# A conditional residual adapter on one core: b2 redistributed, and ScalarE's and VectorE's orders edited

## The chip, the cores and the metric

The kernel runs on one core of one Trainium2 chip. A core has several engines that work side by side, each with its own instruction queue that runs in order: TensorE (PE, matrix products and transposes, with PEld its weight loads), VectorE (DVE), ScalarE (ACT), GpSimd (POOL), and SyncE (SP), which here issues most DMA transfers. They wait for each other by semaphores. Data lies in SBUF; TensorE writes to PSUM, which has eight banks. The metric is the device time of one execution in microseconds (us).

## The reference

For each of 128 batches, x[b] is a matrix of 128 positions by 512 features. A language id picks one of ten adapters:

```
v = itok[b]
h = relu(x[b] @ W1[v] + b1[v])            # 128 x 128
y = x[b] + (h @ W2[v] + b2[v])            # 128 x 512
n = (y - mean(y)) / sqrt(var(y) + 1e-5)   # over the 512 features
out[b] = x[b] + n * gamma[v] + beta[v]
```

All inputs and the output are float32. The tables b2, gamma and beta hold values of their own, so none of these additions may be left out.

## The kernel before

**Set-up.** All tables are brought to SBUF once. W2 lies there for all languages. W1 lies there twice: w1e (lines 159 to 161, two loads) is used for the batches below 24, w1 for the rest (four loads, issued in iterations 12 to 18). The first eight batches have their W1 loaded directly (load_first). The rows of beta, gamma and b2 are spread over 128 partitions by small bf16 matmuls (spread), giving beta_b, gamma_b and b2_b.

**Main loop.** It starts on line 518. Iteration i works on several batches at once, since the steps of a batch are spread over iterations:

- TensorE: transpose_x(i) (four transposes, line 232), down(i-1) (four float32 matmuls, eight in the trace, line 255), up(i-2) (one float32 matmul, two in the trace, line 272). The product of down goes to the one bank of pool p_h, the transposes to the one of p_x, up to one of five banks of p_y, where ys[b] then stays to the end of its batch.
- ScalarE: copy_xT(i) (line 236), relu(i-1) (line 263), square(b) with b = i-3 (line 312; it also sums the squares), after each odd batch deviation (line 322: the root of the pair's variances), and last stage_w1(i+1) (line 223), which copies the W1 of a batch from w1e or w1 to a buffer of its own.
- GpSimd: add_b2 (line 242), r = x + b2, for most batches; add_beta (line 249), o = x + beta, for all.
- VectorE: residual(b) (line 289: y = up + r, with the row sum), and for batches done in pairs: negative_means (line 303), three Newton steps that turn the root into 1/standard deviation (lines 326, 328, 331), scale (line 355: (y - mean) * gamma) and finish (line 364: o = y * rstd + o). With p = g-1, the pair before the current one, the order is for an even batch: residual(b), Newton 1, scale(2p), Newton 2, finish(2p-1). For an odd batch: Newton 3, residual(b), scale(2p+1), negative_means(g), finish(2p).
- SP: loads of x, four batches at a time, and stores of two batches.

**Three ways for b2.** For most batches GpSimd adds b2 to x. For some, TensorE adds it by one more bf16 matmul into the same bank (b2_by_matmul, line 214; line 271 in the trace). For others VectorE adds it in place in a pass of its own (vector_b2, line 282), before residual. Before the change 94 batches go to GpSimd, 11 to TensorE and 23 to VectorE, these mostly four or eight batches apart.

**The order is written by hand.** The function keep (line 45) chains each instruction to the one before on the same engine, so that each engine's order is that of the Python program. Semaphore waits come from the tile framework: it makes an instruction wait for those that wrote what it reads, or that still use a buffer or bank that it takes over.

**Small results in PSUM.** One tile of 64 columns, small, holds a column pair of zeros (for negative_means) and all roots, in slots (smalls, line 295). The last four batches are done singly in tail (line 422), with deviation_of and rstd_of.

Of the kernel before, what the change touches and what calls it, by code (L numbers as in the profile page):

```python
# [8 lines left out]
FP = mybir.dt.float32  # L9
# [3 lines left out]
ALU = mybir.AluOpType  # L13
# [3 lines left out]
P = 128  # L17
G = 4
EPS = 1e-5
FIRST = 8  # L20
# [5 lines left out]
def cond_resid_kernel(ctx: ExitStack, tc: tile.TileContext, x, itok, W1, b1, W2, b2, gamma, beta, out):  # L26
# [8 lines left out]
    nc = tc.nc  # L35
    B, S, H = x.shape
# [8 lines left out]
    def keep(ins):  # L45

        engine = ins.ins.engine
        if engine in last:
            tc.add_manual_dep(ins.ins, last[engine], behind, reason="kept order")
        last[engine] = ins.ins.name  # L50
        return ins
# [7 lines left out]
    st = ctx.enter_context(tc.tile_pool(name="st", bufs=6))  # L59
    p_x = ctx.enter_context(tc.tile_pool(name="p_x", bufs=1, space=PSUM))  # L60
    p_h = ctx.enter_context(tc.tile_pool(name="p_h", bufs=1, space=PSUM))
    p_s = ctx.enter_context(tc.tile_pool(name="p_s", bufs=1, space=PSUM))
# [3 lines left out]
    E = B - 5  # L66
# [144 lines left out]
    xT, hT, rs, os, ys, ssqs, nmeans, rstds = {}, {}, {}, {}, {}, {}, {}, {}  # L211
    phs, pxs, sums = {}, {}, {}

    def b2_by_matmul(b):
        return b < 4 or (b % 4 == 1 and not b2_by_vector(b) and b < E)

    def b2_by_vector(b):
        return b % 4 == 1 and (b % 8 == 5 if b < 24 else b % 32 != 1) and 8 <= b < B - 8

    def stage_w1(b):  # L220
        w1s[b] = wp.tile([P, KC, A], FP, tag="w1s", name=f"w1s_{b}")
        src = (w1e if b < EARLY else w1).rearrange("p l k a -> p (l k a)")[:, bass.ds(lid(b, ET.Activation) * (KC * A), KC * A)]
        keep(nc.scalar.copy(w1s[b].rearrange("p k a -> p (k a)"), src))  # L223
# [10 lines left out]
    def copy_xT(b):  # L234
        xT[b] = tp.tile([P, KC, P], FP, tag="xT", name=f"xT_{b}")
        keep(nc.scalar.copy(xT[b], pxs.pop(b)))  # L236
# [42 lines left out]
    def vector_b2(b):  # L279
        if b2_by_vector(b):  # L280
            v = lid(b, ET.DVE)
            keep(nc.vector.tensor_tensor(ys[b], ys[b], b2_b[:, bass.ds(v * H, H)], ALU.add))  # L282

    def residual(b):
        r = rs.pop(b) if b in rs else xb(b)
        if b % 2 == 0:
            sums[b // 2] = st.tile([P, 2], FP, tag="sum", name=f"sum_{b // 2}")
        keep(
            nc.vector.scalar_tensor_tensor(ys[b], ys[b], 1.0, r, ALU.mult, ALU.add, accum_out=col(sums, b))  # L289
        )  # L290


    small = {}

    def smalls(lo, n):
        if not small:
            small["t"] = p_s.tile([P, 64], FP, tag="s", name="small")
            keep(nc.vector.memset(small["t"][:, 0:2], 0.0))
        return small["t"][:, lo : lo + n]

    def negative_means(g):
        nmeans[g] = st.tile([P, 2], FP, tag="nmean", name=f"nmean_{g}")
        keep(nc.vector.scalar_tensor_tensor(nmeans[g], sums[g], -1.0 / H, smalls(0, 2), ALU.mult, ALU.add))  # L303

    def square(b):

# [27 lines left out]

    def of_pair(g):
        if g not in parts_of:
            parts_of[g] = smalls(8 + 8 * (g % 2), 2), st.tile([P, 2], FP, tag="part", name=f"part_{g}")
        return parts_of[g]

    def deviation(g):  # L340
# [2 lines left out]
    def rstd(g, n):  # L343
        t, u = of_pair(g)
        if n < 3:
            newton(n, ssqs[g], t, u)
        else:
            rstds[g] = st.tile([P, 2], FP, tag="rstd", name=f"rstd_{g}")
            newton_3(rstds[g], t, u)
            del ssqs[g], parts_of[g]  # L350

    def scale(b):
        v = lid(b, ET.DVE)
        keep(
            nc.vector.scalar_tensor_tensor(  # L355
                ys[b], ys[b], col(nmeans, b), gamma_b[:, bass.ds(v * H, H)], ALU.add, ALU.mult
            )
        )
# [12 lines left out]
    def on(b):  # L371
        return 0 <= b < B
# [4 lines left out]

    def of_one(b):
        if -b not in parts_of:
            parts_of[-b] = smalls(32 + 8 * (b % 4), 1), st.tile([P, 1], FP, tag="part", name=f"part_of_{b}")  # L380
        return parts_of[-b]

    def rstd_of(b, n):

        t, u = of_one(b)
        if n < 3:
            newton(n, ssqs[b], t, u)
        else:
            rstds[b] = st.tile([P, 1], FP, tag="rstd", name=f"rstd_{b}")
            newton_3(rstds[b], t, u)  # L390

    def deviation_of(b):
        ssqs[b] = st.tile([P, 1], FP, tag="ssq", name=f"ssq_{b}")
        sq = tp.tile([P, H], FP, tag="sq", name=f"sq_{b}")
        keep(nc.scalar.activation(sq, ys[b], AF.Square, bias=col(sums, b), scale=-float(H), accum_out=ssqs[b]))
        root(ssqs[b], of_one(b)[0])
# [25 lines left out]
    def tail(b):  # L422
        p = E // 2
        residual(b)
        if b == E + 1:
            rstd(p, 1)
            scale(E - 1)
            rstd(p, 2)
            finish(E - 2)
            store(p - 1)  # L430
            rstd(p, 3)
            deviation_of(b)
            shift(E)
            by_pool(E, False)
        elif b == E + 2:
            rstd_of(b - 1, 1)
            negative_means(b // 2)
            rstd_of(b - 1, 2)
            finish_cols(E - 1)
            store_last(E - 1)  # L440
            rstd_of(b - 1, 3)
            store_last(E)
            deviation_of(b)
        elif b == E + 3:
            left, right = slice(0, H // 2), slice(H // 2, H)
            shift(b - 2)
            by_pool(b - 2, False)
            residual(b + 1)
            store_last(b - 2)
            rstd_of(b - 1, 1)  # L450
            scale(b - 1)
            rstd_of(b - 1, 2)
            negative_means(b // 2)
            deviation_of(b)
            scale(b)
            rstd_of(b - 1, 3)
            deviation_of(b + 1)
            by_pool(b - 1, True, left)
            rstd_of(b, 1)
            scale(b + 1)  # L460
            rstd_of(b, 2)
            finish_cols(b - 1, right)
            store_last(b - 1)
            rstd_of(b, 3)
            rstd_of(b + 1, 1)
            finish_cols(b)
            store_last(b)
            rstd_of(b + 1, 2)
            rstd_of(b + 1, 3)
            finish_cols(b + 1)  # L470
            store_last(b + 1)
# [46 lines left out]
    for i in range(3, B + U):  # L518
        b = i - U - 1
        if b > G and b % G == 2 and b // G + 3 < NG:  # L520
            load_x(b // G + 3)
        if i == 5:
            load_x(3)
        if i in (12, 14, 16, 18):
            load_w1((i - 12) // 2)
        if i == 4:
            up(2)
        if i == 5:
            up(3)
        if i > 3 and on(i):  # L530
            transpose_x(i)
        if b <= E:
            add_b2(b + 2)
            add_beta(b)
        if i > 4 and on(i - 1):
            down(i - 1)
        if i > 3 and on(i):
            copy_xT(i)
        if i > 4 and on(i - 1):
            relu(i - 1)  # L540
        if i > 5 and on(i - U):
            up(i - U)


        g, half = divmod(b, 2)
        p = g - 1
        mine, old = 0 <= p < B // 2, 0 <= p - 1 < B // 2
        if b == E:
            add_b2(b + 3)
            add_beta(b + 1)  # L550
            add_b2(b + 4)
            for n in range(b + 2, B):
                add_beta(n)
        if b > E:
            tail(b)
        elif half == 0:
            if on(b):
                residual(b)
            if mine:
                rstd(p, 1)  # L560
                scale(2 * p)
                rstd(p, 2)
            if old:
                finish(2 * p - 1)
                store(p - 1)
        else:
            if on(b):
                vector_b2(b)
            if mine:
                rstd(p, 3)  # L570
            if on(b):
                residual(b)
            if mine:
                scale(2 * p + 1)
            if on(b):
                negative_means(g)
            if mine:
                finish(2 * p)
        if 0 <= b <= E:
            square(b)  # L580
            if half == 1:
                deviation(g)
        if i + 1 >= FIRST and on(i + 1):
            stage_w1(i + 1)

        for n, engine in ((i + 3, ET.Activation), (i - U + 3, ET.PE), (b + 1, ET.DVE), (b + 5, ET.Pool)):
            if on(n):
                lid(n, engine)
# [37 lines left out]
```

## Time and profile before

| What | Value |
|---|---|
| Median of three runs | 311.27 us (310.89 to 311.38) |
| The profiled execution | 311.25 us |
| Its span in the trace | 309.4 us |
| PE busy | 298.0 us (96%) |
| DVE busy | 296.2 us (96%) |
| ACT busy | 280.1 us (91%) |
| POOL busy | 281.4 us (91%) |
| Matmuls of up, per matmul from the trace's group | 256, 598 ns |
| VectorE additions of b2 | 23, 692 ns each |
| Matmuls that add b2 | 11, 380 ns each |

The page gives each engine's busy time, a picture of the span in 40 slices where a digit is the busy share in tenths, the groups of instructions with their durations and idle time, and the waits. The durations of one instruction overlap those of the next, so steps are best read from start to start in the timeline: a matmul row's 275 or 598 ns is longer than the distance to the next matmul. A timeline row holds start, duration, engine, source line, operation, result and operands, and, in brackets, how long the engine was idle before it and which engine or transfer ended that. The granted TensorE clock was full in all stretches up to 300 us.

### The profile page before, as it was taken

The page shows a single profiled execution, that of the slowest core. Times are in us where ns is not written, and L with a number is a line of the kernel's source. Part 1 is how long each engine was busy: PE and PEld are TensorE (multiplying, and loading weights), DVE is VectorE, ACT ScalarE, POOL GpSimd, SP SyncE. Part 2 cuts the span into 40 slices and gives each one's busy share as a digit, 9 for nine tenths or more (in the row PEclk, how much of TensorE's full clock was granted, in tenths as well). Part 3 has the DMA queues.
Part 4 walks back from the last instruction along what each step waited for, and adds up shares of the span by engine and source line. Part 5 has one row for each costly group of instructions (what it writes and reads, how often), then busy time and mean ns, then how long its engine had stood idle before and what let it go on. Part 6 is the DMA issues. An engine that isn't in the chain of part 4 may idle for free. (4 is left out here: it accounts for less than half of the span.)

```text
span 309.4 us, 6966 instructions
## 1 busy us (share of the span) xinstructions
PE 298.0 (96%) x1845; PEld 222.1 (72%) x1845; DVE 296.2 (96%) x827; ACT 280.1 (91%) x716; POOL 281.4 (91%) x235
## 2 busy tenths in 40 slices
PE   8999999999999999999999999999999999999970
PEld 3758778787777777777777777777777777777740
DVE  6787999999999999999999999999999999999994
ACT  3857999999999999999999999999999999999991
POOL 1349999999999999999999999999999999999893
PEclk9999999999999999999999999999999999999995
DMA  7999979986677766666876766677765766882244
GB/s 232 390 387 387 374 225 370 375 278 232 230 271 267 243 210 225 222 233 239 271 249 219 246 202 246 228 250 271 249 225 203 244 237 222 263 271 106 111 159 170
DMA packets 43481, 77.58 MB, mean 251 GB/s; under 512 B 1930, under 2 KB 7061, under 8 KB 43443
## 3 DMA queue, kind: packets, MB, share of 16 engines
q1 hardware_dynamic: 43382, 77.10, 71.9%
q8 instruction: 15, 0.25, 0.3%
q14 instruction: 24, 0.19, 0.2%
q10 hardware_dynamic: 60, 0.05, 0.1%
HBM read 43.58 MB, written 33.55 MB: 249 GB/s over the span
## 5 line engine op out<-in xcount | busy, mean ns | idle before, releaser
L249 POOL TENSOR_TENSOR o<-x,beta_b 128x512 f32<-128x512 f32 x128 | 162.2, 1279 | 9.4 <-DVE beta_b L209 9.4
L255 PE MATMUL ph<-xT,w1s 128*128 128x128 f32 x1024 | 135.4, 275 | 0.0
L242 POOL TENSOR_TENSOR r<-x,b_b 128x512 f32<-128x512 f32 x94 | 120.2, 1279 | 13.1 <-DVE b_b L209 6.2
L272 PE MATMUL py<-w,hT 128*128 x256 | 132.0, 598 | 0.0
L255 PEld LDWEIGHTS ph<-xT,w1s 128*128 128x128 f32 x1024 | 124.9, 192 | 1.0 <-ACT hT L263 0.5
L232 PEld LDWEIGHTS pxT<-ident,x 128*128 128x128 f32 x512 | 66.6, 152 | 65.3 <-issue 35.4
L355 DVE SCALAR_TENSOR_TENSOR py<-py,nmean,gamma_b 128x512 f32<-128x512 f32 x126 | 95.0, 754 | 0.1
L364 DVE SCALAR_TENSOR_TENSOR o<-py,rstd,o 128x512 f32<-128x512 f32 x122 | 91.0, 746 | 0.0
L312 ACT ACTIVATE sq<-py,sum 128x512 f32<-128x512 f32 x124 | 85.2, 687 | 6.1 <-DVE py L289 6.1
L232 PE MATMUL pxT<-ident,x 128*128 128x128 f32 x512 | 78.0, 275 | 0.0
L236 ACT COPY xT<-pxT 128x512 f32<-128x512 f32 x128 | 75.1, 587 | 1.2 <-PE pxT L232 1.2
L289 DVE SCALAR_TENSOR_TENSOR py<-py,r 128x512 f32<-128x512 f32 x94 | 65.1, 693 | 1.4 <-PE py L272 0.7
L223 ACT COPY w1s<-w 128x512 f32 x104 | 63.6, 612 | 0.1
L263 ACT ACTIVATE hT<-ph,b1T 128x128 f32<-128x128 f32 x128 | 47.4, 370 | 6.4 <-PE ph L255 4.3
L272 PEld LDWEIGHTS py<-w,hT 128*128 128x128 f32 x256 | 39.6, 191 | 2.8 <-issue 0.9
L312 ACT ACTIVATION_READ_ACCUMULATOR sq<-py,sum 128x1 f32 x124 | 25.6, 206 | 0.0
L289 DVE SCALAR_TENSOR_TENSOR py<-py,x 128x512 f32<-128x512 f32 x34 | 23.8, 699 | 1.4 <-issue 0.8
L322 ACT ACTIVATE small<-ssq,eps 128x2 f32<-128x2 f32 (+1 forms) x66 | 17.5, 265 | 2.3 <-DVE nmean L303 0.2
L282 DVE TENSOR_TENSOR py<-py,b_b 128x512 f32<-128x512 f32 x23 | 15.9, 692 | 0.0
L289 DVE DVE_READ_ACCUMULATOR py<-py,r 128x1 f32 x94 | 13.3, 142 | 0.0
L326 DVE SCALAR_TENSOR_TENSOR part<-ssq,small 128x2 f32<-128x2 f32 x62 | 9.4, 152 | 1.8 <-ACT small L322 1.8
L223 ACT COPY w1s<-w1e 128x512 f32 x16 | 9.8, 613 | 1.2 <-DMA w1e<-in_L_cond_W_dram 1.1
(54 smaller groups left out, 97.4 us busy)
## 6 DMA issues: line engine op xcount, KB each, us to landing
out_dram<-o SPq DMA_DIRECT2D x61, 512.0 KB, 3.3
x<-in_x_dram SPq DMA_DIRECT2D x29, 1024.0 KB, 6.3
x<-in_x_dram SPq DMA_DIRECT2D x6, 512.0 KB, 8.9
w1e<-in_L_cond_W_dram SPq DMA_DIRECT2D x2, 1280.0 KB, 11.6
w<-in_L_cond_W_dram SPq DMA_DIRECT2D x4, 640.0 KB, 7.5
w1s<-in_L_cond_W_dram SPq DMA_DIRECT2D x8, 256.0 KB, 8.4
w<-in_L_cond_W_dram SPq DMA_DIRECT2D x1, 1792.0 KB, 10.1
out_dram<-o SPq DMA_DIRECT2D x6, 256.0 KB, 2.0
```

The costliest lines, as they stand in the source:

```text
L223: keep(nc.scalar.copy(w1s[b].rearrange("p k a -> p (k a)"), src))
L232: keep(nc.tensor.transpose(pxs[b][:, k, :], cols, ident))
L236: keep(nc.scalar.copy(xT[b], pxs.pop(b)))
L242: keep(nc.gpsimd.tensor_tensor(rs[b], xb(b), b2_b[:, bass.ds(v * H, H)], ALU.add))
L249: keep(nc.gpsimd.tensor_tensor(os[g][:, j, :], xb(b), beta_b[:, bass.ds(v * H, H)], ALU.add))
L255: nc.tensor.matmul(phs[b], lhsT=w1s[b][:, k, :], rhs=xT[b][:, k, :], start=(k == 0), stop=(k == KC - 1))
L263: keep(nc.scalar.activation(hT[b], phs.pop(b), AF.Relu, bias=b1T[:, bass.ds(lid(b, ET.Activation), 1)]))
L272: keep(nc.tensor.matmul(ys[b], lhsT=hT[b], rhs=w2[:, bass.ds(v * H, H)], start=not m, stop=True))
L289: nc.vector.scalar_tensor_tensor(ys[b], ys[b], 1.0, r, ALU.mult, ALU.add, accum_out=col(sums, b))
L312: nc.scalar.activation(sq, ys[b], AF.Square, bias=col(sums, b), scale=-float(H), accum_out=col(ssqs, b))
L355: nc.vector.scalar_tensor_tensor(ys[b], ys[b], col(nmeans, b), gamma_b[:, bass.ds(v * H, H)], ALU.add, ALU.mult)
L364: nc.vector.scalar_tensor_tensor(o, ys.pop(b), rstds[g][:, j : j + 1], o, ALU.mult, ALU.add)
```

## The change

Five edits are made together.

1. The batches are dealt out anew. From batch 24 on, of each sixteen batches three go to VectorE (those with remainder 1, 6 and 11) and one to TensorE (remainder 14). TensorE also gets batches 121 and 123. In all 93 batches go to GpSimd, 15 to TensorE and 20 to VectorE: 13, 21, 27, 33, 38, 43, 49, 54 and so on to 118. Six of the twenty are even batches, so vector_b2 is called for even batches, too, directly before residual.
2. ScalarE's order in an iteration becomes copy_xT(i), stage_w1(i+1), relu(i-1), square(b), deviation.
3. Each Newton step moves behind one more VectorE operation: Newton 1 behind scale(2p), Newton 2 behind finish(2p-1), Newton 3 behind residual of the odd batch.
4. The tile small and its memset are gone. negative_means takes the first two columns of ys[2g+1] as its second operand, with an operation that passes it by. Each root has a tile of its own in the one bank of p_s; those of batches 126 and 127 take the banks of p_h and p_x.
5. In the tail the first Newton step of batch 126 comes before the square of 127, and scale(127) moves behind Newton 3 of batch 126.

```diff
     def b2_by_matmul(b):
-        return b < 4 or (b % 4 == 1 and not b2_by_vector(b) and b < E)
+        return b in (0, 1, 2, 3, 5, E - 2, E) or (b % 8 == 1 if b < 24 else b % 16 == 14 and b < E)
 
     def b2_by_vector(b):
-        return b % 4 == 1 and (b % 8 == 5 if b < 24 else b % 32 != 1) and 8 <= b < B - 8
+        return 8 <= b < B - 8 and (b % 8 == 5 if b < 24 else b % 16 in (1, 6, 11))
...
-    small = {}
-
-    def smalls(lo, n):
-        if not small:
-            small["t"] = p_s.tile([P, 64], FP, tag="s", name="small")
-            keep(nc.vector.memset(small["t"][:, 0:2], 0.0))
-        return small["t"][:, lo : lo + n]
-
     def negative_means(g):
         nmeans[g] = st.tile([P, 2], FP, tag="nmean", name=f"nmean_{g}")
-        keep(nc.vector.scalar_tensor_tensor(nmeans[g], sums[g], -1.0 / H, smalls(0, 2), ALU.mult, ALU.add))
+        keep(
+            nc.vector.scalar_tensor_tensor(
+                nmeans[g], sums[g], -1.0 / H, ys[2 * g + 1][:, 0:2], ALU.mult, ALU.bypass
+            )
+        )
...
     def of_pair(g):
-            parts_of[g] = smalls(8 + 8 * (g % 2), 2), st.tile([P, 2], FP, tag="part", name=f"part_{g}")
+            parts_of[g] = p_s.tile([P, 2], FP, tag="s", name=f"root_{g}"), st.tile([P, 2], FP, tag="part", name=f"part_{g}")
...
     def of_one(b):
-            parts_of[-b] = smalls(32 + 8 * (b % 4), 1), st.tile([P, 1], FP, tag="part", name=f"part_of_{b}")
+            pool, tag = {E + 3: (p_h, "h"), E + 4: (p_x, "xT")}.get(b, (p_s, "s"))
+            parts_of[-b] = pool.tile([P, 1], FP, tag=tag, name=f"root_of_{b}"), st.tile([P, 1], FP, tag="part", name=f"part_of_{b}")
...
             rstd_of(b - 1, 3)
+            rstd_of(b, 1)
             deviation_of(b + 1)
             by_pool(b - 1, True, left)
-            rstd_of(b, 1)
-            scale(b + 1)
             rstd_of(b, 2)
             finish_cols(b - 1, right)
             store_last(b - 1)
             rstd_of(b, 3)
+            scale(b + 1)
...
         if i > 3 and on(i):
             copy_xT(i)
+        if i + 1 >= FIRST and on(i + 1):
+            stage_w1(i + 1)
         if i > 4 and on(i - 1):
             relu(i - 1)
...
             if on(b):
+                vector_b2(b)
                 residual(b)
             if mine:
+                scale(2 * p)
                 rstd(p, 1)
-                scale(2 * p)
-                rstd(p, 2)
             if old:
                 finish(2 * p - 1)
...
             if mine:
-                rstd(p, 3)
+                rstd(p, 2)
             if on(b):
                 residual(b)
             if mine:
+                rstd(p, 3)
                 scale(2 * p + 1)
...
-        if i + 1 >= FIRST and on(i + 1):
-            stage_w1(i + 1)
```

## The prediction

> **What bounds the kernel now.** I read the busy table first, then the slices, then the steps of TensorE (PE) in the timeline, then the waits. Busy shares do not decide: PE and VectorE (DVE) both stand at 96%, and for most of the span at nine tenths or more in every slice.
>
> ```profile
> PE   8999999999999999999999999999999999999970
> DVE  6787999999999999999999999999999999999994
> ```
>
> So I went to the starts of PE's own steps. Per batch it runs T (four transposes, L232), D (eight down matmuls, L255) and U (two up matmuls, L272).
>
> ```profile
> 100.72 1.02 PE L272 MATMUL py<-w,hT 128*128 x2
> ...
> 105.11 1.02 PE L272 MATMUL py<-w,hT 128*128 x2
> 105.97 0.60 PE L232 MATMUL pxT<-ident,x 128*128 128x128 f32 x4
> 106.40 1.06 PE L255 MATMUL ph<-xT,w1s 128*128 128x128 f32 x8
> 107.30 1.02 PE L272 MATMUL py<-w,hT 128*128 x2
> ```
>
> U to U is 6.58 us for three batches, 2.19 a batch: U to T 0.86, T to D 0.44, D to U 0.89 (rounded). From 37.0 to 130.5 us no step is longer than this, apart from T before batch 24 (0.47) and 0.22 for each matmul that adds b2 (91.74 to 91.96). PE is the limit there, and what delays it once there stays. After 130 us it stalls ten times, for instance here:
>
> ```profile
> 139.44 1.06 PE L255 MATMUL ph<-xT,w1s 128*128 128x128 f32 x8
> 140.41 1.12 PE L272 MATMUL py<-w,hT 128*128 x2
> 141.37 0.38 PE L232 MATMUL pxT<-ident,x 128*128 128x128 f32 x2
> ```
>
> D to U is 0.97 and U to T 0.96, so 0.17 is lost, 1.74 over all ten. DVE causes it: four batches take 8.94 (149.88 to 158.82) against PE's 8.76, until U must wait for a bank. Without the b2 addition (L282), which costs 0.67 more (155.41 to the residual at 156.14 is 0.73, where 0.06 stands otherwise), DVE needs 8.27 for four, 2.07 a batch. It falls behind by 0.67 at an addition and recovers 0.12 in each batch without.
>
> **Part 1: b2 dealt out.** Additions on DVE go from 23 to 20, matmuls that add b2 from 11 to 15, GpSimd additions from 94 to 93. DVE saves 3 x 0.67 = 2.0; six of the 20 now stand on even batches, where no Newton step fills the 0.06 between addition and residual, +0.4. These 1.6 are off the path unless DVE is the limit. PE gains 4 x 0.22 = **+0.88** (bounds 0, if all fell into waits, and 0.88; I take 0.88, since PE shows no wait there). With DVE at 16 x 2.07 + 3 x 0.67 + 0.06 = 35.2 per 16 batches and PE at 16 x 2.19 + 0.22 = 35.3, DVE no longer falls behind without end, and the old stalls go: **-1.74** (bounds -1.74 and 0). GpSimd keeps 28 additions per 16 batches, at 1.23 from start to start 34.5, and stays hidden behind PE's 35.3.
>
> **Part 2: the W1 copy ahead of ReLU.** The copy for batch 8 is the first from w1e, and it waits for that load.
>
> ```profile
> 28.22 0.58 ACT L236 COPY xT<-pxT 128x512 f32<-128x512 f32 x1
> 29.11 0.37 ACT L263 ACTIVATE hT<-ph,b1T 128x128 f32<-128x128 f32 x1 [0.31 <-PE ph L255]
> ...
> 31.26 0.62 ACT L223 COPY w1s<-w1e 128x512 f32 x1 [1.11 <-DMA w1e<-in_L_cond_W_dram]
> ```
>
> Today ReLU of batch 6 runs at 29.11, before the wait. Changed, the wait begins at 28.7 and stands in front of it, with square 4 and the next xT copy queued behind. The load was issued by SP at 17.6 and depends on nothing that moves. ReLU 6 starts at 31.26 + 0.52 = 31.78, ends at 32.15, and D of batch 7 may load weights 0.05 later, as it did at 25.69 after the ReLU ending at 25.64. A weight load that waits isn't overlapped: that D took 1.00 to the next U instead of 0.89.
>
> ```profile
> 25.69 1.16 PE L255 MATMUL ph<-xT,w1s 128*128 128x128 f32 x8
> 26.69 0.59 PE L272 MATMUL py<-w,hT 128*128 x1
> ```
>
> So D of batch 7 counts from 32.30, not 30.46: +1.84. The old kernel lost 0.35 right after (U at 31.35 takes 1.06, T at 32.41 0.58, T at 34.75 0.50), which goes. Net **+1.49**. Bounds: the page's median of 11.6 from issue to landing would put it at 29.6, which gives 0.2 - 0.35 = -0.15; a landing 0.1 later than today's gives 1.6. I take the wait's own row. In the steady loop the swap is neutral: the same instructions stand between a square and the next ReLU. SP's and GpSimd's queues keep their order, and every x load and store keeps its place.
>
> **Part 3: the mean reads the batch's own bank.** negative_means (L303) now names the first two columns of the odd batch's ys as an operand that it ignores. It takes 0.15 either way. But as built, the square of every odd batch waits for that mean, where it waited for the residual.
>
> ```profile
> 155.41 0.69 DVE L282 TENSOR_TENSOR py<-py,b_b 128x512 f32<-128x512 f32 x1
> ...
> 156.14 0.70 DVE L289 SCALAR_TENSOR_TENSOR py<-py,x 128x512 f32<-128x512 f32 x1
> ...
> 157.42 0.15 DVE L303 SCALAR_TENSOR_TENSOR nmean<-sum,small 128x2 f32<-128x2 f32 x1
> ```
>
> ```profile
> 156.93 0.69 ACT L312 ACTIVATE sq<-py,sum 128x512 f32<-128x512 f32 x1 [0.34 <-DVE py L289]
> ...
> 157.74 0.27 ACT L322 ACTIVATE small<-ssq,eps 128x2 f32<-128x2 f32 x1
> 157.94 0.60 ACT L223 COPY w1s<-w 128x512 f32 x1
> 158.45 0.57 ACT L236 COPY xT<-pxT 128x512 f32<-128x512 f32 x1
> 158.93 0.37 ACT L263 ACTIVATE hT<-ph,b1T 128x128 f32<-128x128 f32 x1
> ```
>
> Residual to square is 0.79 here. Changed it is 1.28 to the mean, 0.06 for the Newton step now in between, 0.15 for the mean and 0.04 of signal: 1.53. Behind the square on ACT come root, two copies and ReLU, and for that ReLU waits the D after next (one ph bank). Let U of the odd batch start at u. The residual starts at u + 1.13 if DVE is level (40.81 to 41.94), u + 1.86 with an addition ahead. Then square u + 3.39, ReLU 2.00 later at 5.39, weight load at 5.81, with 0.10 for the lost overlap D counts from 5.91. Unhindered it starts at 0.86 + 4.38 + 0.44 = 5.68: 0.23 lost. The old order gives 5.17, no loss. An even addition leaves the next odd batch 0.61 behind: 0.10 lost. Five batches of 0.12 and the stall bring DVE level before the next addition. Twelve odd ones from batch 24 on at 0.225, six even at 0.10, two earlier (slower T) at 0.135: 2.70 + 0.60 + 0.27 = **+3.57**. The old trace shows no such wait, so bounds: 0, if rows are 0.2 shorter than read, and 6.7, if each of the 31 other odd squares from batch 24 to 121 also costs a 0.10 overlap. The row of 0.10 itself is the nearest, so I keep 3.57.
>
> The Trainium skill, page "PSUM — Partial Sum Buffer", section on bank collisions, says that the compiler's scheduler adds a dependency between any two instructions of different engines on one bank, reads against reads included; that speaks against this edit. No row before shows two readers of one bank at once. Priced as a 0.15 instruction alone the edit is free and the sum is 311.85; with the rule's wait it is 315.4.
>
> **Part 4: Newton, root banks, tail.** The first Newton step moves behind scale. Its root, 0.74 later now, ends at residual + 2.6; the step stands at 2.06 + 0.61 + 0.66 = 3.3. No wait. A memset of 0.06 goes at 22.12, where DVE is ahead. A single root bank makes each root wait for the last Newton step of the pair before, which ends before the mean that its square awaits: nothing. In the tail the 0.45 wait at 302.71 (Newton of 126 behind the root of 127) ends, but finish of 125's right half then waits for ScalarE's left half, which by the same rows ends 0.1 earlier than today's 302.61 + 0.45; the work behind it fits as before: **-0.03**, bounds -0.6 (that wait not made) and +0.2.
>
> **Sum.** 311.25 (the profiled execution; span 309.4 and 1.85 around it; 0.02 under the median) + 0.88 - 1.74 + 1.49 + 3.57 - 0.03 = **315.4 us**, 1.3% slower.
>
> **Rivals.**
> A: odd squares don't reach PE. For it: 0.23 is small beside 5.7 of chain. Against: each link is a row. 311.25 + 0.88 - 1.74 + 1.49 - 0.03 = 311.85, at the upper edge of no change.
> B, the other side: DVE sets the pace (20.00 of 20.00 busy from 100 us on), PE's steps can shrink and absorb matmuls and waits. Then only DVE's 1.6 counts: 309.6. It decides if PE can run a batch under 2.19. Against it: 90 us without a shorter step.
> C: ACT becomes the limit, since its slack is small (two batches take it 4.19, 149.51 to 153.70, against PE's 4.38), and each odd square costs: 315.4 + 3.1 = 318.5.
>
> **Numbers.** Forecast 0.62, A 0.17, B 0.11, C 0.10. Its own range, with 0.1 either way at each of the 18 additions, is 313.6 to 317.2; to hold 8 in 10 it reaches over A: 310.9 to 317.4, which leaves out B and most of C. Under 0.2% (0.6 us) this kernel's measurement can't tell from no change: faster 0.12 (B and a little of A), same 0.12 (A), slower 0.76.
>
> **What would show it.** Right: w1s waits about 2.5 us on w1e, directly before a ReLU; waits "ACT sq <- DVE nmean" on odd batches; D with a first step 0.10 longer after odd additions; no D-to-U stretch of 0.97 after 130 us; 15 rows of L271's group. Wrong: T to T at 2.19 through odd additions (A), or under it (B). A landing of w1e near 29.6 would take 1.6 off.

## The result and the profile after

The changed kernel takes 314.99 us (median of four runs, 314.66 to 315.15) against 311.20 us for the kernel before on the same chip: a ratio of 1.0121, 95% interval 1.0104 to 1.0139. It is 1.2% slower. 315.4 was forecast. The profiled execution took 314.66 us, with a span of 312.9 us (309.4 before); lines after the edit are numbered one or a few apart from before (down is L256, up L273, square L309).

The slices of the busy table say no more than they did before: both engines are still at nine tenths nearly everywhere.

```profile
PE   7999899999999999999999999999999999999970
DVE  6877799999999999999999999999999999999995
```

The groups and the table of waits say more. Here a line of a group gives busy time and mean duration, then the idle time ahead of it and who ended that; a line of waits gives the total, how many, and the longest. First the two groups of the page:

```profile
L256 PEld LDWEIGHTS ph<-xT,w1s 128*128 128x128 f32 x1024 | 124.8, 192 | 4.9 <-ACT hT L264 4.2
...
L309 ACT ACTIVATE sq<-py,sum 128x512 f32<-128x512 f32 x124 | 85.7, 691 | 10.7 <-DVE nmean L297 8.6
```

```profile
ACT sq L309 <- DVE nmean L297: 8.6, 20, 0.6
```

The same two groups on the page of the kernel before:

```profile
L255 PEld LDWEIGHTS ph<-xT,w1s 128*128 128x128 f32 x1024 | 124.9, 192 | 1.0 <-ACT hT L263 0.5
...
L312 ACT ACTIVATE sq<-py,sum 128x512 f32<-128x512 f32 x124 | 85.2, 687 | 6.1 <-DVE py L289 6.1
```

A square of an odd batch now waits for the mean, where squares waited for the residual alone before, and the weight loads of down wait 4.2 us for ReLU (0.5 before). Where this happens shows in the starts of TensorE's steps, as before. This is the first of the two places, in the timelines of ScalarE and of TensorE:

```profile
28.51 0.59 ACT L237 COPY xT<-pxT 128x512 f32<-128x512 f32 x1
31.22 0.62 ACT L224 COPY w1s<-w1e 128x512 f32 x1 [2.12 <-DMA w1e<-in_L_cond_W_dram]
31.74 0.36 ACT L264 ACTIVATE hT<-ph,b1T 128x128 f32<-128x128 f32 x1
```

```profile
30.28 0.63 PE L233 MATMUL pxT<-ident,x 128*128 128x128 f32 x4
32.16 1.16 PE L256 MATMUL ph<-xT,w1s 128*128 128x128 f32 x8 [1.24 <-ACT hT L264]
33.15 1.02 PE L273 MATMUL py<-w,hT 128*128 x2
```

The W1 copy waits for the load of w1e, ReLU of batch 6 comes behind it, and D of batch 7 starts 1.88 after the transposes where 0.47 is usual. The transposes of batch 11 start at 38.45; before, at 37.01. So 1.45 us is lost here.

The second place comes back all through the run. Batch 33 gets b2 by VectorE; these are VectorE, ScalarE and TensorE:

```profile
94.94 0.70 DVE L283 TENSOR_TENSOR py<-py,b_b 128x512 f32<-128x512 f32 x1
...
95.67 0.70 DVE L290 SCALAR_TENSOR_TENSOR py<-py,x 128x512 f32<-128x512 f32 x1
...
97.02 0.15 DVE L297 SCALAR_TENSOR_TENSOR nmean<-sum,py 128x2 f32<-128x2 f32 x1
```

```profile
97.21 0.69 ACT L309 ACTIVATE sq<-py,sum 128x512 f32<-128x512 f32 x1 [0.47 <-DVE nmean L297]
...
98.02 0.27 ACT L319 ACTIVATE root<-ssq,eps 128x2 f32<-128x2 f32 x1
98.22 0.58 ACT L237 COPY xT<-pxT 128x512 f32<-128x512 f32 x1
98.70 0.61 ACT L224 COPY w1s<-w 128x512 f32 x1
99.21 0.37 ACT L264 ACTIVATE hT<-ph,b1T 128x128 f32<-128x128 f32 x1
```

```profile
93.87 1.02 PE L273 MATMUL py<-w,hT 128*128 x2
...
97.36 1.06 PE L256 MATMUL ph<-xT,w1s 128*128 128x128 f32 x8
98.25 1.02 PE L273 MATMUL py<-w,hT 128*128 x2
99.11 0.60 PE L233 MATMUL pxT<-ident,x 128*128 128x128 f32 x4
99.63 1.16 PE L256 MATMUL ph<-xT,w1s 128*128 128x128 f32 x8
100.63 1.02 PE L273 MATMUL py<-w,hT 128*128 x2
```

From residual to square it is 1.54 us. The ReLU at 99.21 ends at 99.58, and the D that needs its bank starts at 99.63: 0.52 after its transposes instead of 0.44, and 1.00 to the next U instead of 0.89. Together that is 0.185 us lost, at each of thirteen odd batches with an addition (batch 21, and twelve from 27 on). Elsewhere it is less: 0.10 at batch 13, 0.05 after each of the additions at the even batches 38, 54, 70 and 102, nothing after 118. After the addition at batch 86 it is 0.35. All stalls after 37 us add up to 3.06 us, where the kernel before had 1.73. No D-to-U stretch of 0.97 is left after 130 us.

The last U starts 3.63 us later than before (302.15 against 298.52). The terms give 1.45 + 0.88 (four more matmuls) + 3.06 - 1.73 = 3.66. What comes behind the last U took 10.75 instead of 10.83.

### The profile page after: what moved, and what is told of

It reads as the page before. It is cut to its first block, busy times and chain, and to the rows that moved or that the text cites. A ratio compares the mean times of both kernels' runs of the same rounds, so it can differ in the third digit from the quotient of the medians.

```text
span 312.9 us, 6996 instructions
## 1 busy us (share of the span) xinstructions
PE 299.3 (96%) x1849; PEld 222.7 (71%) x1849; DVE 296.5 (95%) x823; ACT 279.6 (89%) x716; POOL 280.2 (90%) x234
## 5 line engine op out<-in xcount | busy, mean ns | idle before, releaser
L256 PE MATMUL ph<-xT,w1s 128*128 128x128 f32 x1024 | 137.2, 277 | 1.3 <-ACT hT L264 1.2
L273 PE MATMUL py<-w,hT 128*128 x256 | 131.0, 594 | 0.0
L256 PEld LDWEIGHTS ph<-xT,w1s 128*128 128x128 f32 x1024 | 124.8, 192 | 4.9 <-ACT hT L264 4.2
L309 ACT ACTIVATE sq<-py,sum 128x512 f32<-128x512 f32 x124 | 85.7, 691 | 10.7 <-DVE nmean L297 8.6
L290 DVE SCALAR_TENSOR_TENSOR py<-py,r 128x512 f32<-128x512 f32 x93 | 64.4, 693 | 4.4 <-PE py L273 2.6
L224 ACT COPY w1s<-w 128x512 f32 x104 | 64.9, 624 | 0.0
L273 PEld LDWEIGHTS py<-w,hT 128*128 128x128 f32 x256 | 40.0, 192 | 2.1 <-issue 0.9
L290 DVE SCALAR_TENSOR_TENSOR py<-py,x 128x512 f32<-128x512 f32 x35 | 24.5, 699 | 2.1 <-PE py L273 0.9
L309 ACT ACTIVATION_READ_ACCUMULATOR sq<-py,sum 128x1 f32 x124 | 25.9, 209 | 0.0
L319 ACT ACTIVATE root<-ssq,eps 128x2 f32<-128x2 f32 x62 | 16.5, 265 | 2.1
L283 DVE TENSOR_TENSOR py<-py,b_b 128x512 f32<-128x512 f32 x20 | 14.0, 699 | 0.3
L323 DVE SCALAR_TENSOR_TENSOR part<-ssq,root 128x2 f32<-128x2 f32 x62 | 9.3, 149 | 0.8 <-ACT root L319 0.8
```

The source lines that it names most:

```text
L256: nc.tensor.matmul(phs[b], lhsT=w1s[b][:, k, :], rhs=xT[b][:, k, :], start=(k == 0), stop=(k == KC - 1))
L273: keep(nc.tensor.matmul(ys[b], lhsT=hT[b], rhs=w2[:, bass.ds(v * H, H)], start=not m, stop=True))
```

## The experiments

The theory is that the loss has two causes: the first W1 copy in front of a ReLU, and the squares that wait for the mean. The new deal by itself should be worth something. Rivals were that the odd squares don't reach TensorE, that the ScalarE order costs or gains something on its own, and that VectorE sets the pace.

### The mean with another operand that it ignores

The first try removed the dependency by naming an operand in SBUF:

```diff
-                nmeans[g], sums[g], -1.0 / H, ys[2 * g + 1][:, 0:2], ALU.mult, ALU.bypass
+                nmeans[g], sums[g], -1.0 / H, sums[g], ALU.mult, ALU.bypass
```

> The changed kernel, but the mean's ignored second operand is the sums tile in SBUF instead of the odd batch's PSUM bank, so the odd squares wait for the residual alone. Theory (the mean's wait pushes square, ReLU and the D after next): the 18 D steps with a late first weight load after 37 us go, 3.06 us of TensorE stalls with them, and the time falls to 311.9 us. Rival (the stalls come with the additions on VectorE or with ScalarE's new order, whatever the mean reads): the stalls of 0.185 after odd additions stay, 315.0 us.

Measured: 353.45 us (351.85 to 355.09), ratio 1.137 (1.134 to 1.140). As a test of the square's wait it fails, since it changes the price of the mean itself. Its group on this kernel's page (0.15 us each before):

```profile
L297 DVE SCALAR_TENSOR_TENSOR nmean<-sum 128x2 f32<-128x2 f32 x64 | 55.2, 862 | 0.1
```

And two of the 64 in the timeline, VectorE above, GpSimd below:

```profile
149.23 1.18 DVE L297 SCALAR_TENSOR_TENSOR nmean<-sum 128x2 f32<-128x2 f32 x1
...
154.40 1.17 DVE L297 SCALAR_TENSOR_TENSOR nmean<-sum 128x2 f32<-128x2 f32 x1
```

```profile
149.12 1.28 POOL L243 TENSOR_TENSOR r<-x,b_b 128x512 f32<-128x512 f32 x1
...
154.27 1.28 POOL L243 TENSOR_TENSOR r<-x,b_b 128x512 f32<-128x512 f32 x1
```

The mean starts while a GpSimd addition runs and ends when that addition does (150.41 against 150.40; 155.57 against 155.55). So it was in 61 of 64, which ended 15 to 23 ns after the GpSimd row's end; the other three took 0.155 to 0.162 us. The Trainium skill, page "SBUF — State Buffer", section on who interferes with whom, says that a VectorE instruction with two inputs in SBUF contends with a GpSimd instruction that reads SBUF, and that the ports they share are an exclusive lock; the rows agree. 64 x 0.71 = 45 us more VectorE time stands against a span 37 us longer than the changed kernel's (349.7 against 312.9); the 8 us between the two were not broken down. So it matters where the second operand lies, although its values are not used.

The same edit was tried with the first W1 copy moved as well, and failed for the same reason: 353.07 us (348.35 to 353.64), ratio 1.130; its means took 895 ns on average.

```diff
-                nmeans[g], sums[g], -1.0 / H, ys[2 * g + 1][:, 0:2], ALU.mult, ALU.bypass
+                nmeans[g], sums[g], -1.0 / H, sums[g], ALU.mult, ALU.bypass
...
-        if i + 1 >= FIRST and on(i + 1):
+        if i + 1 > FIRST and on(i + 1):
             stage_w1(i + 1)
...
+        if i + 1 == FIRST:
+            stage_w1(i + 1)
```

> Both edits of the two kernels before together on the changed kernel. Theory (the two losses are in series on TensorE, and what is left is four matmuls more, 0.88, against the old kernel's 1.73 us of stalls that are gone): 315.0 - 1.45 - 3.06 = 310.5 us, 0.2% under the old kernel. Rival (the old kernel's stalls return once the new ones are gone, since VectorE falls behind all the same): 312.0 us or more.

The second try keeps the operand in PSUM, but in another bank: the root of the pair before, in the bank of p_s.

```diff
-                nmeans[g], sums[g], -1.0 / H, ys[2 * g + 1][:, 0:2], ALU.mult, ALU.bypass
+                nmeans[g], sums[g], -1.0 / H, (roots.get(g - 1, ys[2 * g + 1]) if g <= E // 2 else ys[2 * g + 1])[:, 0:2], ALU.mult, ALU.bypass
...
-    parts_of = {}
+    parts_of, roots = {}, {}
...
+            roots[g] = parts_of[g][0]
```

> The changed kernel, but the mean of a pair names the root of the pair before as its ignored operand (PSUM, the bank of the roots), so odd squares wait for the residual alone and no instruction of VectorE has two SBUF inputs. Theory (the mean's wait pushes the odd square, ReLU and the D after next): the late first weight loads of D after odd additions go, 3.06 us of stalls after 37 us with them: 311.9 us. Rival (the additions or ScalarE's new order cause the stalls, whatever the mean reads): 315.0 us.

Measured: 312.04 us (311.72 to 312.31, ten runs), ratio to before 1.0023 (1.0014 to 1.0032). The same odd batch in this kernel, VectorE and then ScalarE:

```profile
95.28 0.70 DVE L290 SCALAR_TENSOR_TENSOR py<-py,x 128x512 f32<-128x512 f32 x1
...
96.63 0.16 DVE L297 SCALAR_TENSOR_TENSOR nmean<-sum,root 128x2 f32<-128x2 f32 x1
```

```profile
96.24 0.69 ACT L309 ACTIVATE sq<-py,sum 128x512 f32<-128x512 f32 x1
...
98.25 0.37 ACT L264 ACTIVATE hT<-ph,b1T 128x128 f32<-128x128 f32 x1
```

The square starts 0.96 after the residual, ahead of the mean, and the stalls after 37 us shrink from 3.06 to 0.16. The mean itself costs what it did (0.155 on average; 0.156 in the changed kernel). With one operand's address changed, 2.9 us went: this is the change's largest loss, and its cause is shown.

The same edit of the mean put alone into the kernel before, with its own order and deal:

```diff
-        keep(nc.vector.scalar_tensor_tensor(nmeans[g], sums[g], -1.0 / H, smalls(0, 2), ALU.mult, ALU.add))
+        keep(nc.vector.scalar_tensor_tensor(nmeans[g], sums[g], -1.0 / H, ys[2 * g + 1][:, 0:2], ALU.mult, ALU.bypass))
```

> The old kernel with one edit: the mean's ignored second operand is the first two columns of the odd batch's bank. Theory (the wait of the odd square is enough by itself, in any ScalarE order): each of the 21 odd additions from batch 25 on costs TensorE 0.185, the two earlier ones 0.3 together, and the old 1.73 of stalls after 130 us don't build up: 311.2 + 3.9 + 0.3 - 1.7 = 313.7 us. Rival (the old ScalarE order, with ReLU right behind the xT copy, leaves room): 311.2 us.

Measured: 314.82 us (314.44 to 315.28), ratio 1.0112 (1.0097 to 1.0127). The wait costs more here than expected. Its place is another, too. TensorE, after the addition for batch 37:

```profile
106.28 1.02 PE L272 MATMUL py<-w,hT 128*128 x2
107.31 0.66 PE L232 MATMUL pxT<-ident,x 128*128 128x128 f32 x4
107.80 1.06 PE L255 MATMUL ph<-xT,w1s 128*128 128x128 f32 x8
```

ScalarE of the same kernel:

```profile
105.16 0.69 ACT L312 ACTIVATE sq<-py,sum 128x512 f32<-128x512 f32 x1 [0.50 <-DVE nmean L303]
...
106.17 0.60 ACT L223 COPY w1s<-w 128x512 f32 x1
106.68 0.58 ACT L236 COPY xT<-pxT 128x512 f32<-128x512 f32 x1
```

In the old order the W1 copy stands between the late square and the next xT copy, so the next transposes wait for the bank of p_x: U to T is 1.03 to 1.05 instead of 0.86, and T to D 0.49 instead of 0.44. That is 0.24 us for each of 22 odd additions, 5.42 us with a smaller one at the start, in place of the old stalls of 1.73. In the changed kernel the odd square after an addition starts even later after its U (3.34 us, against 3.26 at batch 37 here), and yet each costs less (0.185). What stands behind the square in ScalarE's order would explain that. No run changed that order alone with the wait in place, so this is read from the rows and not shown by itself.

### The W1 copy

In the changed kernel, only the first W1 copy (batch 8, iteration 7) is moved to the end of its iteration, as before; all others stay ahead of ReLU.

```diff
-        if i + 1 >= FIRST and on(i + 1):
+        if i + 1 > FIRST and on(i + 1):
             stage_w1(i + 1)
...
+        if i + 1 == FIRST:
+            stage_w1(i + 1)
```

> The changed kernel, but the first staged W1 copy (batch 8) stands last in its iteration again, as before; all other W1 copies stay ahead of ReLU. Theory (the copy's wait for w1e holds up ReLU 6 and D of batch 7, and TensorE as the limit never gets it back): the T of batch 11 starts at 37.0 instead of 38.45 us and the time falls by 1.45 to 313.5 us. Rival (the early loss is absorbed later, because VectorE and GpSimd have slack of their own): the time stays at 315.0 within 0.3.

Measured: 313.72 us (313.57 to 314.05), ratio 1.0080 (1.0065 to 1.0095), 1.27 under the changed kernel. ScalarE of this kernel:

```profile
29.13 0.37 ACT L264 ACTIVATE hT<-ph,b1T 128x128 f32<-128x128 f32 x1 [0.31 <-PE ph L256]
29.39 0.68 ACT L309 ACTIVATE sq<-py,sum 128x512 f32<-128x512 f32 x1
...
31.22 0.62 ACT L224 COPY w1s<-w1e 128x512 f32 x1 [1.05 <-DMA w1e<-in_L_cond_W_dram]
```

The load lands when it did, but ReLU is past it. The transposes of batch 11 start at 37.28, 1.17 earlier than in the changed kernel and 0.28 later than before. The stalls after 37 us are as they were except after the addition at batch 13, which now costs 0.26 instead of 0.10. So the profiled executions differ by 1.00 (313.66 against 314.66), while the medians differ by 1.27; that gap lies within the scatter of the runs.

The other way round, the kernel before with all W1 copies put ahead of ReLU and nothing else:

```diff
         if i > 3 and on(i):
             copy_xT(i)
+        if i + 1 >= FIRST and on(i + 1):
+            stage_w1(i + 1)
...
-        if i + 1 >= FIRST and on(i + 1):
-            stage_w1(i + 1)
```

> The kernel before with part 2 alone: every W1 copy ahead of ReLU. Theory: only the first copy from w1e costs, since it then stands in front of ReLU of batch 6, as in the changed kernel (batch 11's transposes there 1.45 later); in the steady loop nothing: 311.2 + 1.45 = 312.7. Rival: the new place costs nothing by itself, 311.2. Second rival: the order also changes the stalls after 37 us (1.73 before), by up to that much: 310.9 if they go as well, over 313.2 if it makes them worse.

Measured: 312.61 us (312.54 to 312.75), ratio 1.0042 (1.0027 to 1.0057). Batch 11's transposes start at 38.46, 1.45 later than before, and the stalls after 37 us are 1.70 against 1.73: the first copy costs, and the order in the steady loop costs nothing by itself.

### Both repairs together

The changed kernel with the mean on the root's bank and the first copy last (the two diffs above):

```diff
-                nmeans[g], sums[g], -1.0 / H, ys[2 * g + 1][:, 0:2], ALU.mult, ALU.bypass
+                nmeans[g], sums[g], -1.0 / H, (roots.get(g - 1, ys[2 * g + 1]) if g <= E // 2 else ys[2 * g + 1])[:, 0:2], ALU.mult, ALU.bypass
...
+        if i + 1 == FIRST:
+            stage_w1(i + 1)
```

> The kernel e9 with the first staged W1 copy last in its iteration, as in e1. Theory (both losses are in series on TensorE): e9 less the 1.27 that e1 measured: 310.7 us, and TensorE's stalls after 45 us under 0.5 us. Rival (with the stalls gone, VectorE falls behind as in the old kernel, and its 1.7 us of stalls come back): 312.0 us or more.

Measured: 311.05 us (310.66 to 311.24, eleven runs), ratio 0.9992 (0.9983 to 1.0001): no change against before that this measurement shows. The two repairs take 3.94 off the changed kernel; alone they took 2.95 and 1.27, which is 4.22. The stalls after 37 us are 0.08, and the last U starts 0.49 earlier than before.

### The new deal

The kernel before with the new deal of b2 alone:

```diff
     def b2_by_matmul(b):
-        return b < 4 or (b % 4 == 1 and not b2_by_vector(b) and b < E)
+        return b in (0, 1, 2, 3, 5, E - 2, E) or (b % 8 == 1 if b < 24 else b % 16 == 14 and b < E)
...
     def b2_by_vector(b):
-        return b % 4 == 1 and (b % 8 == 5 if b < 24 else b % 32 != 1) and 8 <= b < B - 8
+        return 8 <= b < B - 8 and (b % 8 == 5 if b < 24 else b % 16 in (1, 6, 11))
...
+                vector_b2(b)
                 residual(b)
```

> The old kernel with the new distribution of b2 alone, additions on even batches included. Theory (TensorE is the limit: four matmuls more, 0.88, and the 1.73 of stalls after 130 us gone, since VectorE no longer falls behind): 311.3 - 0.85 = 310.4 us. Rival (VectorE sets the pace, its busy time falls by 1.6): 309.7 us. Second rival (TensorE keeps its stalls): 312.2 us.

Measured: 310.34 us (310.04 to 310.64, seven runs), ratio 0.9973 (0.9962 to 0.9984), faster than both kernels. TensorE at a place where the kernel before lost 0.17 (its U at 149.34 there), and at a matmul that adds b2:

```profile
148.32 1.06 PE L255 MATMUL ph<-xT,w1s 128*128 128x128 f32 x8
149.22 1.02 PE L272 MATMUL py<-w,hT 128*128 x2
150.08 0.60 PE L232 MATMUL pxT<-ident,x 128*128 128x128 f32 x4
...
155.79 0.38 PE L271 MATMUL py<-parts,pick 96*128 96x512 bf16 x1
156.01 1.02 PE L272 MATMUL py<-w,hT 128*128 x2
```

D to U is 0.90 and U to T 0.86 again. After 37 us no step of TensorE is late by more than 0.02, and each matmul that adds b2 costs 0.22. The last U starts at 297.73 against 298.52, and 298.52 + 0.88 - 1.73 + 0.08 (batch 11's transposes, a little later) = 297.75. With both repairs the changed kernel still stands 0.7 above this (311.05): its last U starts 0.30 later, and the rest was not broken down. The new places of the Newton steps, the root banks and the tail had no run of their own.

Now TensorE alone is the limit, so the added matmuls should be worth taking back. One kernel gave six of them (batches 30, 46, 62, 78, 94 and 110) to GpSimd, in the kernel with both repairs:

```diff
-        return b in (0, 1, 2, 3, 5, E - 2, E) or (b % 8 == 1 if b < 24 else b % 16 == 14 and b < E)
+        return b in (0, 1, 2, 3, 5, E - 2, E) or (b % 8 == 1 if b < 24 else False)
```

> The kernel e10 with b2 of the seven batches with remainder 14 by sixteen (14 itself is not among them: 30, 46, 62, 78, 94, 110 from batch 24 on) on GpSimd instead of TensorE: six matmuls fewer, six GpSimd additions more. Theory (TensorE is the limit and each matmul that adds b2 costs it 0.22; GpSimd runs some 11 us ahead and can give 6 x 1.23 = 7.4): e10 less 1.3 us, 309.4. Rival (GpSimd, at 29 x 1.23 = 35.8 per sixteen batches against TensorE's 35.1, becomes the limit): not under e10, waits of VectorE on r grow.

Measured: 312.61 us (312.23 to 312.68), ratio 1.0039 (1.0025 to 1.0053), slower than with them. The last U does start earlier, at 297.32 instead of 298.03, but 13.3 us follow it instead of 10.8. GpSimd in the tail, first with both repairs, then with six matmuls less:

```profile
297.79 1.28 POOL L410 TENSOR_TENSOR n<-n,gamma_b 128x512 f32<-128x512 f32 x1 [2.05 <-ACT n L408]
```

```profile
296.23 3.90 POOL L250 TENSOR_TENSOR o<-x,beta_b 128x512 f32<-128x512 f32 x3
299.91 1.44 POOL L410 TENSOR_TENSOR n<-n,gamma_b 128x512 f32<-128x512 f32 x1
```

GpSimd had been ahead by 2.05 us when the tail began. Six more additions of 1.23 use that up, as well as 2.4 of its waits inside the loop (4.3 to 1.9), and its work for the last batches starts 2.1 later. So the deal has a second limit, which no engine's busy share shows: GpSimd's lead at the end.

Two matmuls less (batches 30 and 46), in the kernel before with the new deal:

```diff
-        return b in (0, 1, 2, 3, 5, E - 2, E) or (b % 8 == 1 if b < 24 else b % 16 == 14 and b < E)
+        return b in (0, 1, 2, 3, 5, E - 2, E) or (b % 8 == 1 if b < 24 else b % 16 == 14 and 46 < b < E)
```

> The kernel before with the new deal (310.34) and two of its matmuls that add b2 less: those of batches 30 and 46, whose b2 goes to GpSimd. TensorE saves 2 x 0.22 = 0.44. GpSimd has 3.1 of waits in the loop and 2.2 in the tail of the run with the deal, which is room for two operations of 1.23. Theory: 309.9. Rival: GpSimd comes late in the tail, as with six matmuls less (where the end came 2.5 later after the last up): 310.3 or more.

Measured: 310.01 us (309.81 to 310.56), ratio 0.9964 (0.9951 to 0.9978). The last U starts at 297.29, 0.44 earlier than with the new deal alone, which is two matmuls of 0.22, and 10.8 us still follow it. In the tail, GpSimd still waits 2.22, as in the run with the deal alone:

```profile
297.06 1.28 POOL L411 TENSOR_TENSOR n<-n,gamma_b 128x512 f32<-128x512 f32 x1 [2.22 <-ACT n L409]
```

The two additions went into waits inside the loop: GpSimd's were 4.0 with the deal alone and are 1.6 here. The interval overlaps that of the run before it, so the step between these two rests on the traces. It has the lowest time of all the kernels here.

## Why the prediction was right

The time, the sign and the mechanism came out as forecast, 0.4 us too high. Term by term:

| Term | Predicted | Measured | By |
|---|---|---|---|
| Four more matmuls | +0.88 | 0.22 each | two fewer of them, 0.44 |
| Old stalls | -1.74 | -1.73 | the deal alone: no stall left |
| First W1 copy | +1.49 | +1.45 | the start of batch 11's transposes, also alone |
| Squares waiting for the mean | +3.57 | +3.06 | the stalls; 2.9 of it goes with another bank |
| Newton, root banks | 0 | none put down to them | no run of their own |
| Tail | -0.03 | -0.08 | last U to end |

**The deal.** That VectorE would no longer fall behind was read from its spacing (2.07 a batch, 0.67 an addition) against TensorE's 2.19. The kernel with this part alone has not one stall after 37 us. The part is a gain of 0.9 us, which the other parts hide.

**The W1 copy.** The place and the size were right; taking the wait's own row for the landing, rather than the median of all loads, is what made it so. The copy waited 2.12 and not about 2.5, since the xT copy ahead of it ran 0.3 later than before. D was late all the same, since the load set the end of the wait. Moving this one copy back did not give all 1.45: 0.28 comes back in the iterations right after it, mostly at D of batch 8 (0.79 after its transposes, 0.59 before), and 0.16 after the addition at batch 13. "In the steady loop the swap is neutral" holds as long as squares are on time. Where they are late, the old order lets T wait, and the new one D.

**The squares.** The step that was mis-sized is the start of the chain: "the residual starts at u + 1.13 if DVE is level", read at one place. The addition of batch 33 starts 1.07 after its U (94.94 against 93.87), that of batch 27 1.06 after, and all links behind it were as predicted (0.73 to the residual, 1.35 to the mean, 0.19 to the square, 2.00 to ReLU). With 0.06 less at its head the chain gives 0.17 instead of 0.23 after odd additions and 0.04 instead of 0.10 after even ones; 0.185 and 0.05 were measured. The lost overlap of 0.10 is part of the 0.185, as assumed. The largest miss within the term is one place, D of batch 91 after the addition of 86, at 0.35. There the residual of batch 85 had begun 0.35 late, 1.48 after its U where 1.13 is usual. It begins 1.48 after its U with the mean on another bank, too, so the mean's wait does not make it late; in the kernel before with the new deal alone it is no later than at other such places (1.31). Which part of the change delays it was not found. A smaller stall (0.08, at the transposes of batch 96) remains in that stretch with the mean on another bank. The place gives some 0.30 of the measured 3.06 that the chain doesn't hold; without it the term would have been 0.8 too high instead of 0.5, so part of its closeness is luck.

**The rivals.** A, that the odd squares don't reach TensorE, fell with the run on the root's bank, which gave A's number (312.04; 311.85 worked out) only once the wait was gone. B, that VectorE sets the pace, would have TensorE run under 2.19 a batch; no kernel here shows that, and each matmul less gave 0.22. C, a ScalarE limit with all odd squares, did not come: the other odd squares cost nothing.

## What to carry to other kernels

An operand that an instruction ignores is still an operand: it decides which instructions wait for each other, and it can decide how long the instruction itself takes (862 ns instead of about 155 here). Before naming one, ask who else uses its bank and what is queued behind them, and keep it where it was if both answers are not known. A change of several parts can hide a gain: measured alone, the new deal was faster than either kernel. When work is moved to an engine that seems to have slack, look at its lead where the last work begins, as well as at its busy share.

## What the runs showed of the hardware

The length of a VectorE instruction with two small SBUF inputs was not expected: 862 ns on average instead of 151, because nearly each lasted until the GpSimd addition beside it ended. With one input in PSUM, beside the same GpSimd additions, it took 0.15 to 0.16.

A weight load that has to wait for its bank loses the overlap with the matmul before it. In the D steps after odd additions, and in that of batch 7, the first matmul lasted 0.21 us to the next one instead of 0.11, whether the wait itself had been 0.08 or 1.4: a fixed 0.10, more than half of what each odd addition cost. After even additions the first step took 0.16 with no visible wait, and after the addition at batch 13 it took 0.21 without one, so a part of the overlap can be lost as well.
